# Four stacked cross-attention blocks on one core: a pace table for streams that run side by side, list-schedule durations taken from the trace, and mask terms and context loads at other places

## The chip, the cores and the metric

The kernel runs on one core of one Trainium2 chip. The core has a matrix engine (TensorE, here PE, with its weight loads as PEld), a vector engine (DVE), a scalar engine (ACT), a general engine (POOL) and a queue engine that mostly issues DMAs (SP). The metric is the device time of one execution in microseconds (us), as the median of the runs shown. One execution is also taken by the hardware profiler; durations and waits come from that one. Everything is computed in fp32.

## The reference, cut to what matters

Inputs are a batch of 4 sequences of 512 tokens with width 512 (`x`), a context of 64 tokens for each batch element, and two masks over the context. Four blocks follow each other:

```
x = L0(x, ctx):  two cross attentions (16 heads of 128, softmax over 64 context tokens and one learned key/value),
                 each h = layer_norm(x); x = x + softmax(q k^T) v wo + bo
                 then x = x + gelu(layer_norm(x) w1 + b1) w2 + b2          (w1: 512x2048)
x = L1(x, ctx):  x = x + alpha * softmax(q k^T / sqrt(512)) v wo            (one head)
x = L2(x, ctx):  16 heads of 32 over the 512 own tokens and the 64 context tokens (masked)
                 y = rmsnorm(attention + x); x = gelu(y w1 + b1) w2 + b2 + x
x = L3(x, ctx):  h = layer_norm(x); x = x + attention over the 64 context tokens (16 heads of 32, masked)
                 x = x + gelu(layer_norm(x) w1 + b1) w2 + b2
```

A masked context token gets a large negative term added to its score.

## The kernel before

**What it computes with.** Layer 0 works on tokens in the partitions. For each head, `l0_keys` (L759) makes the keys from the context and multiplies them by the query weights, so that the scores are a product of the normalized tokens with a 512 x 65 operand; `l0_values` (L826) folds values and output weights likewise. `l0_attention` (L888) forms the scores of one batch element, and `l0_tile` (L950) does softmax, transposes (L977) and the product with the folded values. After layer 0, `turn` (L1110) transposes the stream, and the rest works with channels in the partitions. `mlp` (L1034) handles two batch elements at once; its large products are made by `seven` (L1023, matmuls at L1031) with seven products in place of eight and sums on DVE or POOL (`added`, L993). `l2_attention` and `l3_attention` are the attentions of layers 2 and 3; in layer 2, DVE takes the maximum of a score bank (L1522), ACT the exponential (L1534), and PE transposes the result (L1568). `layer_norm` (L1402) is a chain: sums on DVE/POOL, a matmul with the mean (L1412), a subtraction (L1417), a square on ACT (L1398), again sums and a matmul (L1382), root and reciprocal (L1388, L1390), a product (L993) and a scale on ACT (L1423).

**What sets the order.** The order of all engines is made at build time by a class `Plan`, and each engine then runs its instructions in that order, waiting on semaphores. Each step of the kernel is recorded as an `Op` (L194) with a duration for each engine that may do it, for example `pe(2 * MM[512])` or `either(512)` (ACT or DVE). Durations come from formulas (`t_dve`, `t_act`, `t_pool`, L590 to L599) and constants (`MM`, `TR`, `ROWS`, `PAIR`, L602 to L605).

- `beside` (L276) records streams that are to run side by side. `merge` (L285) makes one order of priority of them: it always takes the next op of the stream that has done the smallest share of its own PE time (L332), provided that the live buffers stay under `FULL` blocks.
- `attempt` (L373) is a list schedule with a clock of its own: for each free engine it takes the first ready op by priority, if that lies at most `AHEAD` us of PE time (for loads `AHEAD_LOAD`) ahead of the oldest unfinished op, and if its buffers can be had. An op that has waited for memory for `PATIENCE` blocks that memory for later ones. An op more than 15 us ahead may not take the last `RESERVE` SBUF blocks (L431).
- Where no room is found, `order` (L351) repeats with a lookahead of 20 us around that place.

**The sequence of regions** (L1709 to L1774). For each pair of batch elements and each of the two attentions of layer 0, two halves of eight heads: keys and values run beside each other; in the first half the tokens then follow by themselves (load of a bias row, in the first attention loads of `x`, normalization, transposes L735, sums, and the addition of the bias row to `x` on POOL, L1730); then the attentions. After that five regions: MLP 0 of batches 0, 1 beside layer 1's projections and layer 2's context; MLP 0 of 2, 3 beside attention (layers 1 and 2) of 0, 1; MLP 2 of 0, 1 beside attention of 2, 3 and layer 3's context; MLP 2 of 2, 3 beside layer 3's attention of 0, 1; MLP 3 of 0, 1 beside layer 3's attention of 2, 3. MLP 3 of 2, 3 comes last and alone. Each MLP needs the attention of the region before it, and each attention of layers 2 and 3 the MLP before.

**Ahead of the plan** (L621 to L651), written out directly: the constants, one 512 KB DMA of the whole context on SP (L634), columns and alpha on ACT's queue, two mask loads on POOL's queue (L641, L643), and on DVE the two mask terms (L645, L649), which are read by layers 2 and 3 (L1491, L1371).

Of the kernel before, what the change touches and what calls it, by code (L numbers as in the profile page):

```python
# [192 lines left out]

class Op:  # L194
# [3 lines left out]
class Plan:  # L198
# [9 lines left out]
    PATIENCE = 3.0  # L208

    def __init__(self, sbuf, ahead, ahead_load, reserve, full):  # L210
        self.reserve, self.full = reserve, full * BLOCK
        self.sbuf = Memory(BLOCK, sbuf)
        self.psum = Memory(1024, 4)
        self.ahead, self.ahead_load = ahead, ahead_load
        self.ops, self.regions = [], []
        self.pos = 0.0
# [4 lines left out]
    def ps(self, banks=1):  # L221
        return Buf(self.psum, 512 * banks)

# [61 lines left out]
    def merge(self):  # L285


        ops, last = self.ops, {}
        for op in ops:
            for b in op.uses:  # L290
                last[id(b)] = op
        regions = [[(i, j) for i, j in parts if i < j] for parts in self.regions]
        merged, live, held = [], 0, set()

        def growth(op):
            return sum(b.size for b in op.takes if b.mem is self.sbuf and id(b) not in held)

        def put(op):
            nonlocal live
            for b in op.takes:  # L300
                if b.mem is self.sbuf and id(b) not in held:
                    held.add(id(b))
                    live += b.size
            merged.append(op)

        def drop(op):
            nonlocal live
            for b in op.uses:
                if b.mem is self.sbuf and last[id(b)] is op:
                    live -= b.size  # L310

        at = 0


        for parts in [*regions, [(None, None)]]:
            start = parts[0][0] if parts[0][0] is not None else len(ops)
            for op in ops[at:start]:
                put(op)
                drop(op)
            if parts[0][0] is None:  # L320
                break
            at = parts[-1][1]
            total = [max(sum(o.engines.get("PE", 0.0) for o in ops[i:j]), 1e-9) for i, j in parts]
            next_, gone = [i for i, _ in parts], [0.0] * len(parts)
            readers = {}
            for i, j in parts:
                for op in ops[i:j]:
                    for b in op.uses:
                        readers[id(b)] = readers.get(id(b), 0) + 1
            for _ in range(sum(j - i for i, j in parts)):  # L330
                open_ = [k for k, (_, j) in enumerate(parts) if next_[k] < j]
                open_.sort(key=lambda k: gone[k] / total[k])  # L332
                fit = [k for k in open_ if live + growth(ops[next_[k]]) <= self.full]
                k = fit[0] if fit else min(open_, key=lambda k: growth(ops[next_[k]]))
                op = ops[next_[k]]
                put(op)
                for b in op.uses:
                    readers[id(b)] -= 1
                    if b.mem is self.sbuf and not readers[id(b)]:
                        end = last[id(b)]  # L340
                        if end.n < at:
                            live -= b.size
                next_[k] += 1
                gone[k] += op.engines.get("PE", 0.0)
        self.ops = merged
        pos = 0.0
        for n, op in enumerate(merged):
            op.n, op.pos = n, pos
            pos += op.engines.get("PE", 0.0)
# [23 lines left out]
    def attempt(self, narrow):  # L373
        heaps = {e: [] for e in ("PE", "DVE", "ACT", "POOL", "SP")}
        free_at = dict.fromkeys(heaps, 0.0)
# [3 lines left out]
        events = []  # L379
# [16 lines left out]
        while left:  # L396
            progress = True
            while progress:
# [8 lines left out]
                for e, heap in heaps.items():  # L407
# [5 lines left out]
                    while heap and len(skipped) < 60:  # L413
# [9 lines left out]
                        for m in (self.sbuf, self.psum):  # L423
                            need = [b for b in op.takes if b.mem is m and b.at is None]
                            if not need:
                                continue
                            if m in blocked or not self._fits(m, need):
                                room = False
                                if m not in blocked and now >= op.ready + self.PATIENCE - 1e-9:
                                    blocked.add(m)  # L430
                            elif m is self.sbuf and op.pos > limit + 15.0:  # L431
                                room = room and len(m.free[BLOCK]) > self.reserve
# [169 lines left out]
MM = {512: 0.859, KW: 0.438, 256: 0.432}  # L602
TR = 0.109
ROWS = 1.08
PAIR = 0.96  # L605
# [13 lines left out]
def stack(nc, const, sbuf, psum, a, out):  # L619
# [8 lines left out]
    for i in range(1, 4):  # L628
# [4 lines left out]
    ctxT = const.tile([P, NC, B * T], FP, name="ctxT")  # L633
    nc.sync.dma_start(out=ctxT, in_=a["ctxT"].rearrange("(c p) s -> p c s", p=P))  # L634
# [9 lines left out]
    mterm2 = const.tile([P, B, T], FP, name="mterm2")  # L644
    nc.vector.tensor_scalar(  # L645
        mterm2.rearrange("p b s -> p (b s)"), mk_i, 0.0, -3.0e38, ALU.is_equal, ALU.mult
    )
    mterm3 = const.tile([P, B, T], FP, name="mterm3")
    nc.vector.tensor_scalar(  # L649
        mterm3.rearrange("p b s -> p (b s)"), mk_b, 0.0, LOWEST, ALU.is_equal, ALU.mult  # L650
    )  # L651

    pl = Plan(BLOCKS, AHEAD, AHEAD_LOAD, RESERVE, FULL)
    sb, ps = pl.sb, pl.ps

# [17 lines left out]
    def either(n):  # L673
        return pl.op(ACT=t_act(n), DVE=t_dve(n))
# [32 lines left out]
    def normed(src, scale, offset):  # L707
# [17 lines left out]
        for t in range(NT):  # L725
            n = sb(D)
            with either(D) as o:
                o.affine(n.v(), src[t].v(), rstd[:, t : t + 1], by[:, t : t + 1])
            xn.append(n)
        hT = []  # L730
        for c in range(NC):
            p = ps()
            with pe(4 * TR) as o:
                for t in range(NT):
                    o.transpose(p[:, t * P : (t + 1) * P], xn[t][:, c * P : (c + 1) * P], ident)  # L735
            h = sb(S)
            with either(S) as o:
                o.affine(h.v(), p.v(), col(scale, c), col(offset, c))
            hT.append(h)
# [19 lines left out]
    def l0_keys(n, half, bp):  # L759
# [6 lines left out]
        for j in range(4):  # L766
            for e in range(2):
# [6 lines left out]
                with pe(8 * TR) as o:  # L774
                    mm4(o, p[:, :P], lambda c: wk.v(NC, P)[:, c, :], lambda c: ctxT[:, c, tokens])
                with either(P) as o:
# [4 lines left out]
                for r in range(2):  # L781
                    p = ps()
                    with pe(4 * TR) as o:
# [11 lines left out]
                with pe(2 * TR) as o:  # L795
# [30 lines left out]
    def l0_values(n, half, bp):  # L826
# [6 lines left out]
        for j in range(HH):  # L833
# [5 lines left out]
            with pe(8 * TR) as o:  # L839
                mm4(o, p[:, :P], lambda c: wv.v(NC, P)[:, c, :], lambda c: ctxT[:, c, tokens])  # L840
            with either(P) as o:
# [3 lines left out]
            if j % 2:  # L845
                for i in range(2):
                    p = ps()
                    with pe(PAIR) as o:
# [101 lines left out]
    def l0_tile(half, b, t, sc, U, pb, qs):  # L950
# [14 lines left out]
        with pool(512) as o:  # L965
# [68 lines left out]
    def mlp(layer, pair, hT, func, table, b1, b2):  # L1034
# [23 lines left out]
        for q in range(F // 512):  # L1058
# [4 lines left out]
            def gelu(g, f, src):  # L1063
                g[f] = sb(S)
                with act(S, table) as o:
# [146 lines left out]
    def context_keys(layer, name):  # L1212
# [3 lines left out]
        for d in range(NC):  # L1216
# [3 lines left out]
            with either(256) as o:  # L1220
# [41 lines left out]
    def projected(w, src, name, d):  # L1262
# [5 lines left out]
        with either(S) as o:  # L1268
# [64 lines left out]
    def projected_tiles(name, T, bias, m):  # L1333


        def first(p):
            t = sb(512)
            with either(256) as o:
# [18 lines left out]
    def context_scores(q, kd, t, mterm, b, qs):  # L1357
# [12 lines left out]
        with dve(1024) as o:  # L1370
            o.scalar_tensor_tensor(  # L1371
                sc.v(H, T), p.v(H, T), qs, mterm[:, b : b + 1, :].to_broadcast([P, H, T]), ALU.mult, ALU.add
# [29 lines left out]
    def layer_norm(src, scale, offset):  # L1402
# [17 lines left out]
        for c in range(NC):  # L1420
            added(xc[c].v(), xc[c].v(), r.v(), ALU.mult, S)
            with act(S) as o:
# [6 lines left out]
    def l2_context():  # L1429
# [5 lines left out]
        with pool(256) as o:  # L1435
            o.tensor_tensor(apart[:, 256:].k(1), row[:, 256:], row[:, :256], ALU.subtract)
        bias_steps("L2_xattn_q_b")
# [3 lines left out]
    def l2_attention(b):  # L1441
# [28 lines left out]
        for g in (0, 2, 1, 3):  # L1470
# [6 lines left out]
            for i in range(NT // 2):  # L1477
# [12 lines left out]
                with dve(512) as o:  # L1490
                    o.scalar_tensor_tensor(  # L1491
                        s.v(8, T), p.v(8, T), qs, mterm2[:, b : b + 1, :].to_broadcast([P, 8, T]), ALU.mult, ALU.add
# [8 lines left out]
            for half in range(2):  # L1501
# [3 lines left out]
                for t in (2 * half, 2 * half + 1):  # L1505
# [38 lines left out]
                    with pool(256) as o:  # L1544
# [16 lines left out]
                    with pool(128) as o:  # L1561
# [67 lines left out]
    def l3_context():  # L1629
        row = load_row("L3_xattn_v_b")  # L1630
        bias_steps("L3_xattn_q_b")
        shared3.update(ckT=context_keys(3, "L3_xattn_k_b"), cv=context_values(3, row))

    def l3_attention(b):
# [10 lines left out]
        for t in range(NT):  # L1645
# [13 lines left out]
            with pool(1024) as o:  # L1659
# [50 lines left out]
    for bp, pair in enumerate(pairs):  # L1710
        for n in (1, 2):
            X, pb = {}, {}
            for half in range(2):
                made = {}
                pl.beside(
                    lambda: made.update(keys=l0_keys(n, half, bp)), lambda: made.update(U=l0_values(n, half, bp))
                )
                if not half:
                    row = load_row(f"L0_xattn_bo{n}")
                    for b in pair:  # L1720
                        if n == 1:
                            load_x(b)
                        X[b] = token_sums(normed(x[b], f"L0_xattn_ln{n}_scale", f"L0_xattn_ln{n}_offset"))
                        pb[b] = sb(P)
                        with pool(60) as o:
                            o.memset(pb[b].v(), 0.0)
                    for b in pair:
                        for t in range(NT):
                            with pool(512) as o:
                                o.tensor_tensor(x[b][t].v(), x[b][t].v(), row.v(), ALU.add)  # L1730
# [52 lines left out]
AHEAD, AHEAD_LOAD, RESERVE = 150.0, 60.0, 4  # L1783
FULL = 24
# [56 lines left out]
```

## Time and profile before

| | us |
|---|---|
| median of 3 runs (2820.83 to 2824.44) | 2823.68 |
| the profiled execution's own time | 2821.01 |
| its span, first to last instruction | 2819.2 |
| PE busy (11628 matmul instructions) | 2742.9 |
| DVE busy | 1968.8 |
| POOL busy | 1095.0 |
| ACT busy | 885.8 |
| first matmul starts | 7.37 |
| mean granted PE clock | 0.995 |

An fp32 matmul shows as two instructions. Line numbers are those of the kernel before; a helper's line (L993, L547/L548, L694) stands for many places. In lists of waits, "PE banks L1031 <- ACT arena L1423" means that the matmul at L1031 started when the ACT instruction at L1423 had ended; `arena` is SBUF, `banks` PSUM. By the starts of the matmuls, layer 0's attentions last until about 784 us, MLP 0 of batches 0, 1 until 1018, the next three MLPs' regions until 1508, 2016 and 2306, layer 3's last shared region until 2604, and the last MLP until 2814.

### The profile page before, as it was taken

To read this page: it belongs to the slowest core of one execution; us is meant where nothing else is said; L and a number is where in the kernel's file an instruction comes from. 1 tells how busy PE (TensorE), PEld (TensorE's weight loads), DVE (VectorE), ACT (ScalarE), POOL (GpSimd) and SP (SyncE) were. 2 spreads that over 40 slices of the span, in tenths; PEclk is the share of its full clock that TensorE was granted. 3 is DMA by queue.
4 is the path that set the end of the run, shared out by engine and by line. 5 is a ranking of instruction groups with operands and counts; after the bars stand their busy time and mean duration, and the time that the engine had idled before them with its cause. 6 is when DMAs were issued, how large, how long until landed. Compare 5 with 4: busy or idle time off the path is not lost. (4 is left out here: it accounts for less than half of the span.)

```text
span 2819.2 us, 33561 instructions
## 1 busy us (share of the span) xinstructions
PE 2742.9 (97%) x11628; PEld 1578.9 (56%) x11628; DVE 1968.8 (70%) x3569; ACT 885.8 (31%) x1659; POOL 1095.0 (39%) x1277
## 2 busy tenths in 40 slices
PE   8999999999999999999999999999999989999999
PEld 6667766676654455556554655555454535454444
DVE  6567566675754577777787777678886878687655
ACT  2113122131421114542462355245332213232311
POOL 4234225242322352433235232423744555545431
PEclk9999999999999999999999999999999999999999
DMA  6242142152110220110112012010211110202210
GB/s 198 88 123 65 56 154 86 47 156 83 46 53 30 71 68 8 31 52 24 38 31 79 8 31 71 20 31 16 68 45 45 39 51 30 60 16 67 68 44 30
DMA packets 229832, 163.97 MB, mean 58 GB/s; under 512 B 9072, under 2 KB 198128, under 8 KB 229664
## 3 DMA queue, kind: packets, MB, share of 16 engines
q1 hardware_dynamic: 229296, 161.52, 19.0%
q8 instruction: 93, 1.52, 0.2%
q14 instruction: 75, 0.61, 0.1%
q0 software_dynamic: 80, 0.16, 0.0%
q10 hardware_dynamic: 288, 0.15, 0.0%
HBM read 157.60 MB, written 4.19 MB: 57 GB/s over the span
## 5 line engine op out<-in xcount | busy, mean ns | idle before, releaser
L993 POOL TENSOR_TENSOR arena<-arena 128x256 f32<-128x256 f32 (+3 forms) x828 | 840.0, 1030 | 1119.9 <-ACT arena L547 202.3
L1031 PE MATMUL banks<-arena 128*128 128x512 f32 x2688 | 1212.9, 597 | 18.2 <-ACT arena L1423 12.3
L1031 PEld LDWEIGHTS banks<-arena 128*128 128x128 f32 x2688 | 499.7, 191 | 594.9 <-issue 509.6
L993 DVE TENSOR_TENSOR arena<-arena 128x512 f32<-128x512 f32 (+3 forms) x564 | 449.8, 813 | 69.7 <-ACT arena L1066 16.2
L547 ACT COPY arena<-banks 128x512 f32<-128x512 f32 (+4 forms) x464 | 227.5, 511 | 786.4 <-PE banks L1031 215.6
L548 DVE COPY arena<-banks 128x512 f32<-128x512 f32 (+2 forms) x420 | 253.7, 613 | 189.0 <-PE banks L1031 43.9
L694 PE MATMUL banks<-arena 128*128 128x512 f32 (+2 forms) x944 | 371.1, 542 | 2.3 <-DVE arena L548 0.9
L694 PEld LDWEIGHTS banks<-arena 128*128 128x128 f32 x944 | 167.8, 190 | 180.1 <-issue 167.5
L1066 ACT ACTIVATE arena<-arena,cols 128x512 f32<-128x512 f32 x192 | 137.7, 721 | 358.9 <-DVE arena L1050 176.1
L1050 DVE TENSOR_TENSOR arena<-banks,arena 128x512 f32<-128x512 f32 x240 | 164.4, 686 | 104.1 <-PE banks L1031 94.6
L1309 PE MATMUL banks<-arena 128*128 128x256 f32 x896 | 207.4, 383 | 3.4 <-ACT arena L1423 3.3
L906 PE MATMUL banks<-arena 128*128 128x260 f32 x896 | 208.5, 384 | 0.8 <-ACT arena L547 0.7
L1534 ACT ACTIVATE arena<-banks,arena 128x512 f32<-128x512 f32 x256 | 174.7, 687 | 84.6 <-DVE arena L1524 40.2
L1309 PEld LDWEIGHTS banks<-arena 128*128 128x128 f32 x896 | 170.0, 191 | 54.8 <-issue 23.2
L906 PEld LDWEIGHTS banks<-arena 128*128 128x128 f32 x896 | 164.7, 188 | 38.4 <-issue 5.8
L1522 DVE TENSOR_REDUCE arena<-banks 128x1 f32<-128x512 f32 x256 | 167.5, 680 | 12.0 <-PE banks L1511 9.9
L694 PE MATMUL banks<-ctxT,arena 128*128 128x128 f32 (+1 forms) x1152 | 164.1, 291 | 8.8 <-DMA arena<-in_L_wk 7.4
L1568 PEld LDWEIGHTS banks<-ident,arena 128*128 128x128 f32 x1024 | 116.6, 142 | 88.0 <-ACT arena L1534 32.8
L694 PEld LDWEIGHTS banks<-ctxT,arena 128*128 128x128 f32 x1152 | 148.5, 194 | 27.5 <-issue 13.6
L1568 PE MATMUL banks<-ident,arena 128*128 128x128 f32 x1024 | 140.6, 278 | 12.1 <-ACT arena L1534 11.5
L1089 DVE TENSOR_TENSOR arena<-banks,arena 128x512 f32<-128x512 f32 x144 | 98.7, 686 | 46.0 <-PE banks L1031 45.7
L985 DVE TENSOR_TENSOR arena<-banks,arena 128x512 f32<-128x512 f32 x64 | 44.2, 690 | 117.0 <-PE banks L694 114.1
(154 smaller groups left out, 2518.6 us busy)
## 6 DMA issues: line engine op xcount, KB each, us to landing
arena<-in_L_w SPq DMA_DIRECT2D x192, 256.0 KB, 3.1
arena<-in_L_wk SPq DMA_DIRECT2D x80, 256.0 KB, 4.8
arena<-in_L_wqT SPq DMA_DIRECT2D x64, 256.0 KB, 5.4
arena<-in_L_wv SPq DMA_DIRECT2D x64, 256.0 KB, 5.4
arena<-in_L_wo SPq DMA_DIRECT2D x64, 256.0 KB, 5.5
arena<-in_L_wq SPq DMA_DIRECT2D x32, 256.0 KB, 4.6
arena<-in_L_wo SPq DMA_DIRECT2D x8, 1024.0 KB, 6.0
arena<-in_L_wv SPq DMA_DIRECT2D x6, 1024.0 KB, 5.7
```

What stands on the lines that cost most here:

```text
L547: "ACT": lambda e, out, in_: e.copy(out, in_),
L548: "DVE": lambda e, out, in_: e.tensor_copy(out, in_),
L694: o.matmul(dst, lhs(c), rhs(c), start=(c == 0), stop=(c == NC - 1))
L906: o.matmul(p[:, : 2 * KP], lhs(c), rhs(c, b % 2), start=(c == 0), stop=(c == 1))
L993: o.tensor_tensor(out, x, y, op)
L1031: o.matmul(p.v(), lhs(c), rhs(c), start=(c == 0), stop=(c == 1))
L1050: o.tensor_tensor(t.v(), p.v(), y.v(), ALU.add)
L1066: o.activation(g[f].v(), src.v(), func, bias=col(b1, q * NC + f))
L1309: o.matmul(p[:, i * 256 : (i + 1) * 256], lhs(c), rhs(c), start=(c == 0), stop=(c == 1))
L1522: o.tensor_reduce(m[:, i : i + 1].k(i), banks[i].v(), AX.X, ALU.max)
L1534: o.activation(y.v(), banks[i].v(), AF.Exp, bias=nm[:, i : i + 1].k(i), scale=qs, accum_out=sums[:, i : i + 1].k(i),)
L1568: o.transpose(p[:, c * P : (c + 1) * P], e[i][:, c * P : (c + 1) * P], ident)
```

## The change

It leaves all matmuls, evictions and sums as they are and changes how they are put in order, and a few places.

1. **Pace table.** Each stream of a region gets 17 numbers: where it is to stand (in hundredths) when it has done 0/16, 1/16 ... 16/16 of its PE time. `merge` takes the stream that stands lowest. With a straight line for every stream this would be the old rule.

```
+        def stands(pace, share):
+            at = min(max(share, 0.0), 1.0) * 16
+            i = min(15, int(at))
+            lo, hi = pace[i] / 100.0, pace[i + 1] / 100.0
+            return lo + (hi - lo) * (at - i)
...
-                open_.sort(key=lambda k: gone[k] / total[k])
+                open_.sort(key=lambda k: stands(self.paces[n][k], gone[k] / total[k]))
```

Of the 13 regions' entries, the first and the last three (MLP first, then attention; in the first: keys, values, tokens):

```
+PACES = [
+    [
+        [0, 3, 16, 19, 24, 28, 34, 39, 45, 51, 55, 57, 67, 77, 80, 88, 96],
+        [8, 12, 12, 20, 24, 30, 38, 45, 50, 56, 61, 66, 69, 80, 98, 111, 114],
+        [0, 1, 8, 16, 25, 31, 38, 44, 51, 57, 64, 72, 79, 89, 90, 95, 101],
+    ],
...
+    [
+        [0, 7, 13, 19, 25, 31, 38, 43, 50, 56, 63, 69, 75, 81, 88, 94, 99],
+        [-3, 5, 13, 18, 24, 29, 37, 48, 50, 56, 63, 69, 75, 70, 87, 93, 99],
+        [-11, -5, -1, 3, 8, 10, 23, 34, 40, 45, 49, 54, 69, 83, 84, 84, 90],
+    ],
+    [
+        [0, 6, 21, 11, 24, 35, 37, 45, 49, 58, 59, 67, 72, 79, 80, 92, 96],
+        [12, 6, 15, 20, 32, 37, 46, 31, 32, 28, 48, 50, 57, 69, 82, 80, 89],
+    ],
+    [
+        [-8, -9, -7, -5, 10, 15, 23, 37, 45, 51, 62, 79, 81, 92, 97, 113, 120],
+        [-14, -14, -8, -4, 15, 22, 32, 38, 26, 39, 47, 46, 60, 92, 89, 74, 99],
+    ],
+]
```

2. **Planner's numbers.** The list schedule's engines begin at times of their own instead of 0, and five limits change:

```
+    BEGIN = {"PE": 1.0, "DVE": 3.0, "ACT": 3.0, "POOL": 3.2, "SP": 0.8}
...
-AHEAD, AHEAD_LOAD, RESERVE = 150.0, 60.0, 4
-FULL = 24
+AHEAD, AHEAD_LOAD, RESERVE = 90.0, 98.0, 2
+FULL = 22
...
+PATIENCE, NEAR = 1.75, 35.0
```

`PATIENCE` was 3.0, and `NEAR` takes the place of the 15 us beyond which the reserve holds.

3. **Durations.** Matmuls with 65 x 4 columns 0.444 instead of 0.438; short matmuls of layer 0's keys and values 0.112 (`SHORT`) instead of 0.109; an eviction with a bias 0.09 us more on ACT and half of that on DVE, one with scale and bias 0.17 and half of that; the gelu at L1066 0.725; the scale at L1423 0.81; the POOL products L966 1.06, L1545 0.62, L1562 0.3, L1660 1.92; the value pairs L850 0.04 more.

4. **Tokens of layer 0 beside keys and values.** What stood by itself after the first half's region becomes a function and a third stream of that region; its content is the same:

```
+                streams = [
+                    lambda: made.update(keys=l0_keys(n, half, bp)),
+                    lambda: made.update(U=l0_values(n, half, bp)),
+                ]
+                pl.beside(*streams, *([] if half else [l0_tokens]))
```

5. **Context in two halves, through the plan.** `ctxT` and the mask terms are fixed tiles that the plan now knows (class `Held`, which takes and gives no memory), so that their writers are ops like others. The 512 KB DMA ahead of the plan goes; for each pair of batches there is a load of its 128 context tokens:

```
-    nc.sync.dma_start(out=ctxT, in_=a["ctxT"].rearrange("(c p) s -> p c s", p=P))
...
+        two = slice(bp * P, (bp + 1) * P)
+        load(ctxT[:, :, two].k(bp), chunks(a["ctxT"])[:, :, two], NC * P)
```

6. **Mask terms.** The two DVE instructions at L645 and L649 go from the head of the kernel into `l2_context` and `l3_context`, as ops of the plan:

```
+        with dve(256) as o:
+            o.tensor_scalar(mterm2, mk_i.rearrange("p (b s) -> p b s", b=B), 0.0, -3.0e38, ALU.is_equal, ALU.mult)
...
+        with dve(256) as o:
+            o.tensor_scalar(mterm3, mk_b.rearrange("p (b s) -> p b s", b=B), 0.0, LOWEST, ALU.is_equal, ALU.mult)
```

The loads of the masks themselves stay on POOL's queue at the head.

## The prediction

> **What bounds the kernel now.** I read the busy shares first, then who PE waits for, then the granted clock at those waits, then the stages.
>
> The page's busy times and its slices (each digit a tenth of a fortieth of the span):
>
> ```profile
> PE 2742.9 (97%) x11628; PEld 1578.9 (56%) x11628; DVE 1968.8 (70%) x3569; ACT 885.8 (31%) x1659; POOL 1095.0 (39%) x1277
> ...
> PE   8999999999999999999999999999999989999999
> ```
>
> PE is busy for 2742.9 of 2819.2 us; no other engine is near. DMA moves 58 GB/s in the mean, and 275 to 305 in the first 40 us. So only time in which PE does nothing, or runs slowly, can be won. The page shows 76.3 us of it, but a matmul that ends before a wait counts as busy until its modelled end. So I also took, from the trace's starts, the time from one matmul's start to the next, and subtracted the lower quartile of the same group (0.429 us for 512 columns, 0.216 for 256, 0.109 to 0.112 for 128). The floor is 2665.1 us, 143.7 us are lost between matmuls, 7.4 pass before the first and 4.7 after the last. Of the 143.7, 94.5 lie in 142 waits of over 0.15 us; the other 49 are crumbs that an order hardly reaches.
>
> Who PE waited for (waiter, releaser, us in total, times, longest):
>
> ```profile
> PE banks L1031 <- ACT arena L1423: 12.3, 2, 9.5
> PE banks L1568 <- ACT arena L1534: 11.5, 14, 2.3
> PE banks L694 <- DMA arena<-in_L_wk: 7.4, 1, 7.4
> PE banks L1511 <- ACT arena L1534: 7.0, 8, 1.5
> PE banks L1382 <- POOL arena L993: 3.8, 1, 3.8
> PE banks L1309 <- ACT arena L1423: 3.3, 3, 2.2
> ```
>
> Two kinds matter. L1423 and L1382 are the ends and the middle of a layer norm: the next region's MLP (L1031) has to wait for it. L1534 is an exponential of layer 2's attention, for which the transposes L1568 wait, often and briefly. L694 is the very first matmul.
>
> The stages, with PE's busy time as second number (length, then PE, PEld, DVE, ACT, POOL, granted clock, DMA):
>
> ```profile
> 0.00:54.70 54.70, 43.93 (x296) 33.77 (x297) 29.50 (x70) 13.78 (x29) 15.51 (x46) 1.00 0.74 232
> 54.70:784.00 729.30, 724.08 (x3672) 495.55 (x3671) 470.65 (x988) 184.22 (x349) 268.07 (x381) 1.00 0.30 90
> 784.00:1038.00 254.00, 252.95 (x715) 127.84 (x714) 143.83 (x224) 40.31 (x59) 87.92 (x77) 1.00 0.16 50
> 1038.00:2016.00 978.00, 947.71 (x4836) 545.13 (x4835) 738.00 (x1541) 428.47 (x919) 353.12 (x448) 1.00 0.13 39
> 2016.00:2604.00 588.00, 568.90 (x1599) 283.99 (x1598) 452.94 (x566) 175.14 (x242) 302.92 (x273) 0.99 0.15 42
> 2604.00:2819.20 215.20, 205.29 (x518) 92.59 (x516) 133.87 (x184) 43.89 (x65) 67.43 (x57) 0.99 0.15 47
> ```
>
> By starts the six lose 9.8, 24.2, 2.4, 64.6, 31.6 and 9.4 us (rounded, 142), and their waits over 0.15 us are 4.6, 7.6, 1.7, 45.4, 27.0 and 8.2. Layer 0 (to 784) is nearly closed. Two thirds lie from 1038 on, where MLP and attention run beside each other.
>
> The worst place, the chain at the border between the last two shared regions, by PE's lines of the timeline:
>
> ```profile
> 2314.21 1.13 PE L1412 MATMUL banks<-arena,mean 128*128 128x512 f32 x2
> ...
> 2324.87 10.67 PE L1031 MATMUL banks<-arena 128*128 128x512 f32 x19 [9.53 <-ACT arena L1423]
> ```
>
> Two of the stretches that I asked for, in the columns of the stages:
>
> ```profile
> 2319.20:2329.40 10.20, 4.53 (x6) 1.95 (x7) 9.79 (x10) 4.30 (x6) 8.99 (x7) 0.50 0.00 0
> 2489.90:2493.20 3.30, 3.30 (x10) 2.59 (x9) 2.45 (x4) 0.00 (x0) 2.59 (x3) 0.50 0.00 0
> ```
>
> The MLP of batches 2, 3 and the attention of 0, 1 end together at 2314; then nothing is left for PE while a layer norm runs through ACT, DVE (a reciprocal of 3.34 us) and POOL. PE idles 9.53 us and gets half the clock until 2329.4. After a wait of 2.22 us at 2488 the clock is halved too, for 3.4 us. There are six such stretches: near 1456, 1828, 2029, 2319, 2490, 2626. Five of 3.4 us cost 1.7 each, the long one, in which PE ran from 2324.9, 2.3: 10.8 us.
>
> **The change, part by part.**
>
> *Work itself.* No matmul, eviction or sum is added or removed; one DMA is added (the context in two). So the floor of 2665.1 us stays, and the sum is about lost time alone.
>
> *Start.* The first matmul waits until 7.37 us for a weight that queues behind all 512 KB of context; half of that is now loaded later. 256 KB at the 275 GB/s of the first 20 us are 0.95 us. The two mask terms (L645, L649; 0.29 us each) leave DVE's queue: the second waits 0.99 us for its mask and starts at 10.06, and the first key's shift (L553) stands behind it at 10.27, though its matmuls end at 9.41: 0.7 us with the 0.2 that such a step takes. They go beside the MLP of 784 to 1038, where DVE is busy 143.8 of 254 us: nothing there; without that cover 0.3 us each. The second context half is one SP issue (0.4 to 0.5 us) amid 256 KB loads, needed about 400 us later: nothing. l0_tokens becomes a third stream: it takes along a row load and, for the first pass, eight loads of x (256 KB each, 5.6 us of SP issue now at 27.8), eight statistics on DVE (L713), eight POOL additions (1.32 us each) per pass and the transposes L735. Now its DVE and ACT work falls in 40 to 60 us, where DVE is busy 17.7 of 20 and PE idles 1.8; earlier it finds DVE at 11.3 of 20. Against it: 2.3 MB earlier among weights when DMA is busy 0.93 is 7.5 us of transfer in front of weights at 305 GB/s. Bounds: the stage loses 9.8 us and 7.4 before it, of which at best half goes, -8; at worst two thirds of the 7.5 come through, +5. The weights still lead in the pace table (third stream at 0, 1, 8 against 0, 3, 16 where low goes first), so I am near the gain: **-4**.
>
> *Rest of layer 0.* The waits of L977, L694, L735 (up to 1.0 us) around 451 to 461 and 647 are where tokens now stand alone. They add to 7.6 us; half goes: **-4** (0 to -8). 784 to 1038: **0**.
>
> *Borders from 2016 on.* The pace table lets attention run ahead: in the region of the MLP of layer 3, its attention's last point is 99, where the MLP passes 99 at share 0.88; in the region before, 89 against 0.92. An MLP is 448 matmuls of 0.429, 192 us, so 23 and 15 us of MLP remain as cover, against a chain of 23.6 us (2301.3 to 2324.9), of which 9.5 was bare. What goes if the cover holds: waits of 9.70, 4.01, 2.90, 2.38, 1.05 and 1.05 by starts, 21.1, and 7.4 of clock (2.3 and three times 1.7): 28.5. I take three quarters, since the attention that goes ahead leaves less beside the MLP's own short waits: **-22** (-33 to +5).
>
> The clock is shown by the rows above. [...]
>
> *Layer 2's attention, 1038 to 2016.* Waits of 45.4 us in 74 places, mean 0.6, and 3.4 of clock within. Here gain comes from a finer order: durations now like the rows (0.725 for the gelu, row L1066 721 ns; 1.06 for L966, row 1051; 0.112 for short matmuls; 1.92 for L1660, row 1956), a shorter patience, other paces. Bounds: nothing or +10, where an instruction is put ahead of one that is then late; -40, nearly all waits. What limits it is that the same form still varies: L993 on POOL with 512 columns takes 1456 ns in the mean, L966 of the same width 1051, so an order exact to 0.1 us isn't kept. I take 45%: **-20**.
>
> *Lookahead 150 to 90, loads 60 to 98, FULL 22, reserve 2.* 90 us of PE work still exceeds the 23.6 us chain; loads land in 3.1 to 8.1 us against 60 already: **0**.
>
> Sum: -4 - 4 - 20 - 22 = -50. Span 2819.2 - 50 = 2769.2; the profiled execution has 1.8 us around it (2821.0): 2771.0. The median before, 2823.68, is 2.7 above that execution: **2773.7, say 2773 us**, 1.8% faster.
>
> **The rivals.**
>
> *A: borders alone.* The fine waits come back elsewhere, because DVE (738 of 978 us) and the shared exponentials set the pace from 1038 to 2016. For: 14 waits of L1568 on L1534, each ended by ACT right behind DVE. Against: ACT is busy 428 of 978 us, so a head start of one tile would do. Gain 4 + 22 = 26 with little else: 2798 (2790 to 2816).
>
> *B: nearly closed.* All waits over 0.15 us but a fifth go: 0.8 x 94.5 = 75, plus start: 2745 (2728 to 2757).
>
> *C: the table changes little.* Priority alone moves, PE is 97% busy, and the ready list gives the same order: 2823 (2818 to 2829).
>
> *D: slower, by memory.* With reserve 2 instead of 4 and loads 98 us ahead, the planner runs out of room in some place and repeats with a lookahead of 20 us there; the 23.6 us chain then lies bare at six places, as many as have a halved clock now: 9.5 + 2.3 at each is 70.8, less the 28.5 and the 8.2 (2.43, 2.35, 3.4) lost there now, is +34: 2858. It decides once four places or more are so hit. Against: FULL falls from 24 to 22 blocks, which asks for less. A milder case gives 2830 to 2840.
>
> **How the numbers follow.** Forecast (2757 to 2790) 0.46; A 0.22; B 0.19; C 0.05; D 0.08. Faster by over 0.2% (about what a measurement of this kernel can tell from no change) is all of the first three: 0.87; C 0.05; D 0.08. The range leaves out C, D and the lower part of B (0.06): 2738 to 2816.
>
> **What would show it.** Right: PE's floor the same; the waits on L1423 and L1382 under 8 us in total instead of 19.4; at most two half-clock stretches after 1000 us; first matmul near 6.4 us; L906 starting before 52 us; lost time from 1038 to 2016 near 45 us. Wrong: a new wait of PE on a DMA of wk in the first 60 us (the tokens' loads), L1568's and L1511's waits still above 15 us (A), or long waits at new borders (D). A floor that moves, through the clock or missing overlap of packed matmuls, would break the whole sum.

## The result and the profile after

The changed kernel takes 2774.5 us in the median (2771.5 to 2778.5 in four runs), the kernel before beside it 2822.64; the ratio is 0.983 with a 95% interval of 0.9813 to 0.9847. The forecast was 2773. The profiled execution took 2772.95 us, its span is 2771.1. In lines after the change L1031 is L1054, L1423 is L1446, L1382 is L1405, L1412 is L1435, L1534 is L1559, L1568 is L1593, L1511 is L1536, L694 is L717, L993 is L1016.

The page of the changed kernel, busy times and PE's slices:

```profile
PE 2730.7 (99%) x11628; PEld 1578.9 (57%) x11628; DVE 1929.8 (70%) x3516; ACT 889.5 (32%) x1663; POOL 1144.9 (41%) x1325
...
PE   8999999999999999999999999999999999999999
```

The same 11628 matmuls stand in a span that is 48 us shorter. By the starts of the matmuls, with the quartiles of the kernel before, the floor is again 2665.1 us; lost between matmuls are 95.3 us instead of 142 (2819.2 less the floor, 7.4 in front and 4.7 behind; the 143.7 of the prediction is 1.7 too much). The waits of over 0.15 us are 92 with 50.9 us instead of 142 with 94.5.

Who PE waited for, longest first:

```profile
PE banks L717 <- DMA arena<-in_L_wk: 6.0, 1, 6.0
PE banks L1536 <- ACT arena L1559: 4.7, 6, 2.0
PE banks L1054 <- ACT arena L1559: 4.0, 3, 2.3
PE banks L1593 <- ACT arena L1559: 3.5, 5, 1.4
PE banks L717 <- DVE arena L737: 3.2, 1, 3.2
PE banks L1435 <- POOL arena L1016: 1.4, 1, 1.4
```

The waits on the end and the middle of a layer norm (19.4 us before) have gone from the head of the list. Behind the first weight, the exponentials are now first, and there is a new wait of 3.2 us at the start. The view puts it down to a statistic of the tokens (L737). But these are the matmuls of the first value weight `wv`, whose load is issued behind a row and four loads of `x` (the queue is shown below) and lands at 14.49 us (the second key's weight lands at 17.59); the matmuls start at 14.63. In e4, with the same order on the queue, the same wait is put down to that load:

```profile
PE banks L717 <- DMA arena<-in_L_wv: 4.0, 1, 4.0
```

The stages of the changed kernel, cut where the same work ends:

```profile
0.00:56.40 56.40, 45.42 (x288) 34.05 (x288) 32.33 (x74) 18.54 (x37) 25.20 (x50) 1.00 0.97 295
56.40:782.00 725.60, 725.21 (x3697) 498.69 (x3694) 457.24 (x993) 175.46 (x334) 270.23 (x391) 1.00 0.30 89
782.00:1033.00 251.00, 250.87 (x684) 124.75 (x683) 145.90 (x213) 38.00 (x57) 90.57 (x81) 1.00 0.18 52
1033.00:1993.00 960.00, 942.46 (x4853) 548.27 (x4853) 722.36 (x1511) 430.25 (x929) 360.12 (x464) 1.00 0.13 37
1993.00:2562.00 569.00, 564.93 (x1601) 281.33 (x1600) 446.80 (x556) 191.68 (x255) 331.42 (x291) 1.00 0.16 45
2562.00:2771.10 209.10, 201.82 (x515) 91.81 (x513) 125.20 (x174) 35.57 (x53) 67.33 (x53) 1.00 0.13 41
```

A table by equal work is sharper. I sum the floor over the matmuls in order and compare the times at which 37.6, 742.6, 994, 1908 and 2665 us of it are done (the ends of the start, layer 0, the first MLP, layer 2's attention, and all). Each column is the time gained (-) or lost in that stretch against before, in the profiled executions (which lie up to 4 us beside their medians). The last two are the median against the changed kernel's, and what the kernel's own list schedule reckons at build time against the same (the planner's clock, not a measurement).

| run | median | start | layer 0 | MLP | 994 to 1908 | from 1908 | median, vs 2774.5 | planner |
|---|---|---|---|---|---|---|---|---|
| changed | 2774.5 | +2.7 | -5.8 | -1.8 | -18.2 | -25.0 | | |
| e1 straight paces, last two | 2777.4 | +1.9 | -5.9 | -1.7 | -11.9 | -22.6 | +2.9 | +1 |
| e2 table shifted, a | 2794.0 | +0.4 | -5.8 | -1.6 | +2.5 | -21.7 | +19.5 | +24 |
| e3 table shifted, b | 2819.3 | -0.8 | -3.9 | -1.8 | +14.8 | -7.8 | +44.8 | +46 |
| e4 old limits | 2817.5 | +2.7 | -5.9 | -1.6 | -3.6 | +6.1 | +43.0 | +40 |
| e5 old reserve rule | 2804.1 | +2.2 | -5.8 | +0.7 | -10.8 | -3.9 | +29.6 | +31 |
| e6 before, new reserve rule | 2802.8 | +0.3 | -5.7 | +0.9 | -1.8 | -12.0 | | |
| e7 old durations | 2778.4 | +3.0 | -10.2 | -1.3 | -18.6 | -15.9 | +3.9 | |
| e8 first tokens alone | 2773.2 | -4.0 | -4.8 | -2.2 | -14.4 | -23.1 | -1.3 | +1 |
| e9 no table | 2793.2 | +1.4 | -2.9 | -0.3 | -2.2 | -23.1 | +18.7 | +25 |
| e10 context and masks alone | 2814.5 | -1.1 | -3.0 | +0.8 | -1.1 | -1.6 | | |
| e11 searched on | 2767.0 | -4.6 | -6.5 | -2.0 | -23.4 | -21.6 | -7.5 | -13 |
| e12 old rule for loads | 2807.2 | +1.0 | -4.8 | -2.0 | -5.4 | -1.1 | +32.7 | +32 |

### The profile page after: what moved, and what is told of

Its sections match the earlier page's. It is cut to its first block, busy times and chain, and to the rows that moved or that the text cites. A ratio compares the mean times of both kernels' runs of the same rounds, so it can differ in the third digit from the quotient of the medians.

```text
span 2771.1 us, 33551 instructions
## 1 busy us (share of the span) xinstructions
PE 2730.7 (99%) x11628; PEld 1578.9 (57%) x11628; DVE 1929.8 (70%) x3516; ACT 889.5 (32%) x1663; POOL 1144.9 (41%) x1325
## 5 line engine op out<-in xcount | busy, mean ns | idle before, releaser
L1016 POOL TENSOR_TENSOR arena<-arena 128x256 f32<-128x256 f32 (+3 forms) x876 | 887.8, 1029 | 1089.5 <-DVE arena L576 202.1
L1054 PE MATMUL banks<-arena 128*128 128x512 f32 x2688 | 1203.8, 595 | 7.4 <-ACT arena L1559 4.0
L1054 PEld LDWEIGHTS banks<-arena 128*128 128x128 f32 x2688 | 497.4, 190 | 584.5 <-issue 508.2
L575 ACT COPY arena<-banks 128x512 f32<-128x512 f32 (+3 forms) x489 | 242.7, 513 | 786.4 <-PE banks L1054 277.6
L1016 DVE TENSOR_TENSOR arena<-arena 128x512 f32<-128x512 f32 (+3 forms) x516 | 419.2, 824 | 70.1 <-POOL arena L1016 20.3
L717 PE MATMUL banks<-arena 128*128 128x512 f32 (+2 forms) x944 | 368.2, 542 | 0.3
L576 DVE COPY arena<-banks 128x512 f32<-128x512 f32 (+3 forms) x395 | 237.1, 607 | 163.1 <-PE banks L1054 49.8
L717 PEld LDWEIGHTS banks<-arena 128*128 128x128 f32 x944 | 167.8, 190 | 180.3 <-issue 173.9
L1559 ACT ACTIVATE arena<-banks,arena 128x512 f32<-128x512 f32 x256 | 174.7, 687 | 96.5 <-DVE arena L1549 55.1
L717 PE MATMUL banks<-ctxT,arena 128*128 128x128 f32 (+1 forms) x1152 | 167.4, 294 | 10.2 <-DMA arena<-in_L_wk 6.0
L717 PEld LDWEIGHTS banks<-ctxT,arena 128*128 128x128 f32 x1152 | 149.6, 195 | 33.0 <-issue 13.1
L1593 PEld LDWEIGHTS banks<-ident,arena 128*128 128x128 f32 x1024 | 118.0, 142 | 77.5 <-issue 34.8
L1593 PE MATMUL banks<-ident,arena 128*128 128x128 f32 x1024 | 140.0, 276 | 4.7 <-ACT arena L1559 3.5
```

Of the source, the lines that this page charges most:

```text
L575: "ACT": lambda e, out, in_: e.copy(out, in_),
L576: "DVE": lambda e, out, in_: e.tensor_copy(out, in_),
L717: o.matmul(dst, lhs(c), rhs(c), start=(c == 0), stop=(c == NC - 1))
L1016: o.tensor_tensor(out, x, y, op)
L1054: o.matmul(p.v(), lhs(c), rhs(c), start=(c == 0), stop=(c == 1))
L1559: o.activation(y.v(), banks[i].v(), AF.Exp, bias=nm[:, i : i + 1].k(i), scale=qs, accum_out=sums[:, i : i + 1].k(i),)
```

## The experiments

**Do the paces cover the borders?** Theory 1 is the prediction's: attention runs ahead of the MLP and leaves it as cover. Theory 2: the table is fitted to one order, and the order as a whole is what counts.

e1, straight lines in the last two shared regions:

```
+PACES[11:] = [[[100 * i / 16 for i in range(17)] for _ in r] for r in PACES[11:]]
```

> The changed kernel with straight paces in the last two shared regions (MLP 2 of batches 2, 3 and MLP 3 of 0, 1, each beside layer 3's attention). Theory 1, as predicted: the paces there let attention run ahead and so cover the layer norm; without them the waits on the layer norm's end and some halved clock come back, 15 to 25 us: 2790 to 2800 us. Theory 2: the gain at the borders comes from the order as a whole (lookahead, reserve, durations), and the paces there matter little: 2770 to 2780 us, PE's waits on the norm's end still under 8 us.

2777.4 us (ratio 0.9839, 0.9824 to 0.9854). From 1908 on 22.6 of the 25.0 us remain. In the changed kernel attention did lead: its last norm's first matmul stands 18.7 and 29.9 us ahead of the MLP's last matmul at the two borders, 3.9 and -0.4 before. In e1 the leads are again 3.9 and -0.4, and the borders are closed all the same. Theory 1, by which the leads are needed, falls.

e2 and e3, each number of the table moved by -2 to +2 (two draws; e3 differs in the seed alone):

```
+_r = random.Random(1)
+PACES = [[[p + _r.choice((-2, -1, 0, 1, 2)) for p in t] for t in r] for r in PACES]
```

> The changed kernel with every number of the pace table moved at random by -2 to +2 hundredths. Theory 1, the table expresses which stream should lead and when: so small a shift keeps the covers, and the time stays within 6 us of 2774.5. Theory 2, the table is fitted to one order, and what it gains lies in the fit, not in a rule: half or more of the 48 us goes, 2795 to 2815 us, with the loss spread over many short waits and not at the borders. The kernel's own planner reckons 24 us more than for the changed kernel.

> The same with another draw of -2 to +2 hundredths. Theory 1: within 6 us of 2774.5. Theory 2: as the last, and as the kernel's planner reckons 46 us more than for the changed kernel, near 2815 to 2825; if the planner's clock says nothing of the chip, this run and the one before fall in either order.

2794.0 (0.9898, 0.9883 to 0.9912) and 2819.3 (0.9992, 0.9983 to 1.0002). e2 is a little better than its forecast of 2795 to 2815. A shift that leaves the two leads about as they were (17.0 and 30.6 us in e2, 24.1 and 31.5 in e3) costs 19.5 and 44.8 us, nearly all of it from 994 to 1908 in e2, and there and behind in e3. The order of loss is that of the planner's clock.

**Are the limits worth nothing?** e4, the changed kernel with the five limits of before and 15 us for `NEAR`:

```
-AHEAD, AHEAD_LOAD, RESERVE = 90.0, 98.0, 2
-FULL = 22
-PATIENCE, NEAR = 1.75, 35.0
+AHEAD, AHEAD_LOAD, RESERVE = 150.0, 60.0, 4
+FULL = 24
+PATIENCE, NEAR = 3.0, 15.0
```

> The changed kernel with the limits of before (lookahead 150, loads 60, reserve 4, FULL 24, patience 3, 15 us). Theory 1: the limits are worth nothing by themselves, as predicted: 2770 to 2782 us. Theory 2: any limit is part of the fit, and the planner reckons 40 us more: 2805 to 2820 us.

2817.5 (0.9979, 0.9969 to 0.9988): 43 us more, 31 of them from 1908 on. PE's matmuls at the border of e4, and the granted clock there:

```profile
2291.70 15.37 PE L1054 MATMUL banks<-arena 128*128 128x512 f32 x35
2309.30 1.12 PE L1435 MATMUL banks<-arena,mean 128*128 128x512 f32 x2 [2.23 <-POOL arena L1016]
2319.81 2.07 PE L1405 MATMUL banks<-arena,mean 128*128 128x512 f32 x2 [9.39 <-POOL arena L1016]
2321.68 10.88 PE L1054 MATMUL banks<-arena 128*128 128x512 f32 x22
```

```profile
2311.00:2324.00 13.00, 4.19 (x5) 1.80 (x6) 12.83 (x12) 3.11 (x5) 10.79 (x9) 0.50 0.00 1
```

Attention leads by 18.4 us here, as in the changed kernel, and yet PE idles 9.39 us at half the clock: the lead alone isn't the cover. So theory 3: the rule on the last SBUF blocks decides. An op more than `NEAR` us ahead may not take them, and the next MLP's weights and sums are such ops.

e5, only that rule as before; e6, the kernel before with three numbers alone, the rule's two and the lookahead (`AHEAD`):

```
e5:
-AHEAD, AHEAD_LOAD, RESERVE = 90.0, 98.0, 2
+AHEAD, AHEAD_LOAD, RESERVE = 90.0, 98.0, 4
...
-PATIENCE, NEAR = 1.75, 35.0
+PATIENCE, NEAR = 1.75, 15.0
e6:
-                            elif m is self.sbuf and op.pos > limit + 15.0:
+                            elif m is self.sbuf and op.pos > limit + 35.0:
...
-AHEAD, AHEAD_LOAD, RESERVE = 150.0, 60.0, 4
+AHEAD, AHEAD_LOAD, RESERVE = 90.0, 60.0, 2
```

> The changed kernel with only the reserve rule of before: the last 4 blocks of SBUF, not 2, are kept from ops more than 15 us, not 35, ahead. Theory 3, formed from the last four runs (old limits bring the half clock at the borders back, straight paces there don't): the borders are bare because the ops that could cover them lie more than 15 us ahead and are refused memory. Then the stretch from 1900 us on loses 15 to 25 us more, with halved clock again near 2290 to 2480: 2795 to 2808 us. Theory 2 (fit only): a loss of any size, not at the borders in particular. Theory 1: nothing, under 2782 us. The kernel's planner reckons 31 us more than for the changed kernel.

> The kernel before with three numbers alone: 15 us to 35, reserve 4 to 2, lookahead 150 to 90. No pace table, old durations, tokens and context as before. Theory 3: the borders from 2000 us on gain 8 to 15 us and the whole 15 to 25, without any table: 2797 to 2808 us. Theory 2: the limits are worth something only with the table fitted to them: within 6 us of 2822. The planner reckons 21 us less than for before.

2804.1 (0.9938, 0.9923 to 0.9953) and 2802.8 (0.993, 0.9914 to 0.9947), both as theory 3 had it. e5 loses 21 us of the 25 from 1908 on, e6 gains 12 there and 19.3 in all, with no table at all. What the lookahead adds in e6 no run separates.

**What is worth the rest?** e9, everything changed but the table (straight paces everywhere; FULL 23, since at 22 the planner finds no room):

```
+PACES = [[[100 * i / 16 for i in range(17)] for _ in r] for r in PACES]
-FULL = 22
+FULL = 23
```

> The changed kernel with straight paces in all 13 regions (each stream at its own share, the old rule) and FULL at 23, since the planner finds no room at 22; limits, durations, tokens, context and masks as changed. Theory 3 (the reserve rule closes the borders, the table only finds a good order elsewhere): from 1900 us on the gain over before stays at 15 to 25 us, attention leads the MLP at the border by no more than before (near 4 us), and what is lost against the changed kernel lies between 1000 and 1900 us: 2792 to 2802 us. Theory 1 (the table's leads are the cover): the borders are bare again, from 1900 us on no gain, 2810 us and more.

2793.2 (0.989, 0.9874 to 0.9907). From 1908 on the gain stays whole at 23.1, with leads of 3.9 and -0.4; from 994 to 1908 it is 2.2 instead of 18.2. PE at the border of e9:

```profile
2292.32 1.02 PE L1435 MATMUL banks<-arena,mean 128*128 128x512 f32 x2
2293.17 8.75 PE L1054 MATMUL banks<-arena 128*128 128x512 f32 x20
2301.76 1.02 PE L1405 MATMUL banks<-arena,mean 128*128 128x512 f32 x2
2302.61 1.97 PE L1054 MATMUL banks<-arena 128*128 128x512 f32 x4
2304.42 1.02 PE L1435 MATMUL banks<-arena,mean 128*128 128x512 f32 x2
2305.28 12.18 PE L1054 MATMUL banks<-arena 128*128 128x512 f32 x28
```

Up to 2304 this is the sequence of the kernel before (x20, x4, then the next norm at 2314). There PE then had nothing; here it has 28 more. They belong to the next MLP, though the norm of its batch 1 isn't done: two of the seven products of `seven`, a11 b11 and a12 b21, need batch 0 alone, and there is such a pair for each block of `w1` in SBUF (by the plan's order, the 28 also hold the first product of two blocks of `w2`, whose input needs batch 0 alone).

The changed kernel gets over the same border in another way. These are the last scales of batch 1's norm on ACT, before, in the changed kernel, in e9 and in e4:

```profile
2323.30 1.52 ACT L1423 ACTIVATE arena<-arena,cols 128x512 f32<-128x512 f32 x2 [0.70 <-DVE arena L993]
2277.77 1.52 ACT L1446 ACTIVATE arena<-arena,cols 128x512 f32<-128x512 f32 x2 [0.17 <-POOL arena L1016]
2312.68 1.52 ACT L1446 ACTIVATE arena<-arena,cols 128x512 f32<-128x512 f32 x2 [0.16 <-POOL arena L1016]
2300.48 1.52 ACT L1446 ACTIVATE arena<-arena,cols 128x512 f32<-128x512 f32 x2 [0.16 <-POOL arena L1016]
```

The last matmul of MLP 2 of 2, 3 starts at 2305.6, 2276.4, 2296.2 and 2299.4. So the norm ends 19.2 us behind it before, 2.9 us in the changed kernel, 18.0 in e9 and 2.6 in e4 (0.6 in e5). In the changed kernel the lead does bring the norm in time, and by the plan's order the third product behind the border, s4 b22, already uses batch 1. e9 (like e1) does without it. e4 and e5 have the norm and stay bare, because sums on POOL come late: 9.39 us of wait in e4, 5.86 in e5.

I also counted in the traces the weight loads of the MLPs issued by 10 us before the last matmul of MLP 2 of 2, 3, beyond that MLP's own: 6 before, 2 in e4, 8 in e5, 6 in e6 and e10; 14 in the changed kernel, 10 in e1, 12 in e9. And L1054's instructions in the 20 us behind that matmul: 17 before, 16 in e4, 28 in e5, 27 in e6, 29 in e10; 39, 42 and 42.

e12, the old rule for the loads alone:

```
-                            elif m is self.sbuf and op.pos > limit + self.near:
-                                room = room and len(m.free[BLOCK]) > self.reserve
+                            elif m is self.sbuf and op.pos > limit + (15.0 if op.load else 35.0):
+                                room = room and len(m.free[BLOCK]) > (4 if op.load else 2)
```

> The changed kernel with the old reserve rule (15 us, 4 blocks) for the weight loads alone; the computing ops keep the new one. Theory 3, narrower: what the old rule withholds at the borders is the next MLP's weights, so that its first sums come late; then the stretch from 1900 us on loses 12 to 22 us again: 2795 to 2810 us. If the rule acts through the computing ops alone, the borders stay closed, and what is lost (a new draw) lies before 1900 us.

2807.2 (0.9946, 0.9929 to 0.9962); from 1908 on 23.9 of the 25.0 us are gone, a little over the forecast, but not at that border: 38 instructions of the MLP stand in those 20 us, with 6 loads ahead. So the count of loads doesn't tell whether a border is covered. By the same sum, the work that lay from 2290 to 2345 us before gains 10.0 us in the changed kernel and 8.8 in e12, 1.9 in e5, and loses 3.2 in e4. e5 and e12 differ in the rule for the computing ops alone, so at that border the old rule acts through the computing ops, the sums among them, rather than through the loads. (e10, with the old rule throughout, gains 5.7 there: another order does a part of it too.) What e12 loses lies elsewhere, at waits on another norm's end (4.4 us) and on DVE (4.8 us). Whether the loads that are kept back cause it, or another order, isn't shown.

e7, the durations of before in the planner (the eleven constants and formulas of point 3 put back):

> The changed kernel with the durations of before in the planner, all else as changed. If the durations matter on the chip by themselves, the order that the planner finds with the old ones, though it looks as good to the planner (by its old clock), runs worse: 8 to 20 us more, 2783 to 2795 us, mainly in short waits on the exponentials between 1000 and 2000 us. If they don't: 2770 to 2780 us, or a loss like that of the shifted tables, since any other order is a new draw.

2778.4 (0.9845, 0.983 to 0.986), 3.9 more, within what another order may do. The new durations are worth little by themselves.

**The start.** e8, tokens by themselves in the first region only; e10, the kernel before with context halves and mask terms alone:

```
e8:
-                pl.beside(*streams, *([] if half else [l0_tokens]))
+                pl.beside(*streams, *([] if half or not (n + bp > 1) else [l0_tokens]))
+                if not half and n + bp == 1:
+                    l0_tokens()
```

> The changed kernel with the tokens by themselves in the very first region only, as before; the seven others stay as changed. The trace of the changed kernel shows four loads of x and a row between the first weights, the statistics on DVE ahead of the second key's shift, and PE 5.5 us behind the kernel before at equal work (10 us of it). If those loads are the cause, at 10 us of PE work it is 4 to 6 us earlier, and with a later order as good as the changed one: 2768 to 2774 us. If the cause is the slow clock alone, the start stays as it is.

> The kernel before with only the context in two halves through the plan and the mask terms in layers 2 and 3: straight paces, old limits, old durations, tokens by themselves, engines beginning at 0. As predicted for this part, the first matmul is 1.0 to 1.5 us earlier and the first key's shift 0.7 more: at 37.6 us of PE work 1 to 2 us gained, nothing later but what a slightly different order brings: 2816 to 2825 us. Theory 2 would call even the rest a new draw, of up to 10 us either way.

e8: 2773.2 (0.9827, 0.9813 to 0.9842). The start is 6.7 us better than in the changed kernel, and about 6 of it are given back later, in another order. e10: 2814.5 (0.9971, 0.9959 to 0.9983), 8 us less than before and under its forecast of 2816 to 2825: 1.1 us of it lie at the start, as forecast; the other 5 that its profiled execution shows lie in small steps in a different order, of which I have no cause.

The changed kernel's SP queue and PE at the start:

```profile
1.80 0.50 SPq L701 DMA_DIRECT2D arena<-in_L_wqT  x1
2.34 0.44 SPq L701 DMA_DIRECT2D arena<-in_rows  x1
2.82 4.20 SPq L701 DMA_DIRECT2D arena<-in_x  x4
7.06 1.43 SPq L701 DMA_DIRECT2D arena<-in_L_wv  x1
```

```profile
6.03 2.05 PE L717 MATMUL banks<-ctxT,arena 128*128 128x128 f32 x8 [6.03 <-DMA arena<-in_L_wk]
8.90 2.07 PE L808 MATMUL banks<-arena 128*128 128x130 f32 x8 [0.82 <-DMA arena<-in_L_wqT]
10.77 0.64 PE L819 MATMUL banks<-arena,cols 128*128 128x130 f32 x2
14.63 2.05 PE L717 MATMUL banks<-ctxT,arena 128*128 128x128 f32 x8 [3.22 <-DVE arena L737]
```

The first matmul is 1.3 us earlier, but a row and four loads of x go out behind the first key's two weights and ahead of all others, the first value's matmuls start at 14.63 instead of 11.71, and eight still take 2.05 us where they take 1.05 at full clock (from 26.59 on; granted clock 1.00).

**A faster version.** e11 starts from e8 and changes the table further in small random steps, keeping what lowers the planner's clock (patience 2.25).

> The first region's tokens by themselves, as in the eighth run, and the pace table changed further in small random steps, each kept when the planner's own clock fell; patience 2.25, other limits as changed. The planner reckons 14 us less than for the eighth run (2773.2 us). Theory 2 in full (the time follows the planner's clock, whatever the numbers of the table mean): 2757 to 2763 us, with the gain between 1000 and 1900 us. If the planner's clock is worth nothing at this scale: 2768 to 2778 us.

2767.0 us (0.9803, 0.9788 to 0.9817), the fastest here, 55 us under the kernel before beside it. That lies between its two forecasts (2757 to 2763, and 2768 to 2778). Its four runs (2763.0 to 2768.9) lie below all four of the changed kernel, though the two intervals of the ratio overlap. Against e8 it won 6 of the 14 us that the planner reckoned, 9 of them between 994 and 1908, with some given back behind.

## Why the prediction was right, and where it wasn't

- **Floor:** unchanged, 2665.1 us. Right.
- **Start, -4:** wrong in sign, +2.7. The parts on context and masks held (first matmul at 6.03 against some 6.4, first shift at 8.12 instead of 10.27; e10's -1.1). The step that failed is "The weights still lead in the pace table, so I am near the gain". The numbers given beside it say the opposite: the lowest goes first, and the tokens' 0, 1, 8 lie below the keys' 0, 3, 16 and the values' 8, 12, 12; and a row, loads of x and statistics have no PE time, so they don't move their stream on at all. SP's queue shows row and x in front of `wv`. With the tokens by themselves (e8) the start is -4.0; so taking them along costs 6.7 us, over the bound of 5 that I had set.
- **Rest of layer 0, -4; first MLP, 0:** -5.8 and -1.8. Right in mechanism, the first a little small.
- **Borders, -22:** the size was right (-25.0), the cause only in part. The pace table does give the leads that I worked out (18.7 and 29.9 us against 15 and 23), and in the changed kernel the norm ends in time at the first of them (2.9 us behind the MLP instead of 19.2). But the leads are not needed, since e1 and e9 close the borders without them, and not enough, since e4 leaves the border bare with them. The step that failed is the one put at nothing, "Lookahead 150 to 90, loads 60 to 98, FULL 22, reserve 2": the limits cost 43 us when undone (e4), the reserve rule alone 29.6 (e5), and three numbers give the kernel before 19.3 (e6). I had set 90 us against a chain of 23.6 and not asked what an op beyond 15 us may take from memory.
- **Layer 2's attention, -20:** -18.2, and 46.4 us lost there against the 45 forecast. The reason "durations now like the rows" failed (e7). The table brings it (e9 has 2.2 without), but as one order found by fitting: a shift of two hundredths takes all of it and more (e2, e3).
- **Rival D, memory:** its condition came, its price didn't. The plan of the changed kernel does run out of room and repeats with the lookahead of 20 us, five times around four places, all in layer 2's attention (1083 to 1783 us of PE work); the plan of the kernel before never does. The norms' chains at the borders lie elsewhere, so the +34 stayed away; what the repeats cost in layer 2's attention no run separates. The rule that D feared, with its smaller reserve, is the main gain.
- Of the signs named, the waits on the norm, one halved stretch after 1000 us beside the last, and the first matmul came as said; L906 before 52 us did not (56.4). Of the signs of being wrong, a new wait on a weight behind the tokens' loads came too, though on `wv` and not on `wk`.

So 2773 against 2774.5 is partly luck: an error of 6.7 us at the start is made up by 3.0 at the borders, 1.8 in the rest of layer 0, 1.8 in the MLP and the rounding, less 1.8 in layer 2.

What stays open: e3 loses 17 us behind 1908 with the new rule in force, half of it at the border at 2010, where a wait of 8.8 us follows and only 12 instructions of the MLP stand in the 20 us behind, so an unlucky order can cost there too; the rule is the main cause by the sum of the runs (with it -7.8 to -25.0 in nine kernels, the one before as base 0; with the old one, in e12 for the loads alone, -3.9 to +6.1 in four). Which withheld op is the decisive one at the other borders isn't settled, nor what reserve and distance (`NEAR`) are worth each. e4 costs 13 us more than e5: the other limits have no run of their own, and neither have `BEGIN` and the tokens of the later regions.

## What to carry to other kernels

When a hand-made list schedule leaves the main engine bare at a stage border, ask first what the scheduler's memory rules keep from being fetched ahead, and count in the trace how many of the next stage's matmuls run in the first 20 us behind the border. The number of its loads that are out didn't tell here (6 with 17 matmul instructions, 6 with 38), and a stream's lead was of no use without the sums that the next stage starts from. A table fitted to one order is worth what the fit finds, and a shift of 2% in it undid 19.5 and 44.8 of 48 us here, so judge such a table by a disturbed copy as well. Loads that a step takes along belong behind those that the first busy engine waits for (ahead of them, the tokens' cost 6.7 us here, by e8).

## What the runs showed of the hardware that I had not expected

Whether a wait of PE of 2 to 3 us was followed by a lower clock was not the same at every place. In the kernel before, four waits of 2.18 to 2.73 us, which ended at 1454.72, 1826.45, 2488.48 and 2626.11, were each followed by half the clock for 3.41 us, as was one of 3.84 us that ended at 2028.75; around one of 9.53 us that ended at 2324.87 it was half for 10.24 us, from 2319.20 on. In the changed kernel's profile a wait of 2.01 us on an exponential, which ended at 1938.17, was followed by half the clock for 3.41 us from 1938.44, and one of 2.29 us on another, which ended at 1424.67, was not (1.00 from 1424 to 1428). The changed kernel's four runs took 2771.5, 2772.95, 2776.05 and 2778.47 us with mean granted clocks of 1.000, 0.999, 0.998 and 0.997. What decides whether such a wait costs clock isn't shown.

At the start, the record of the granted clock begins, at full speed, at 15.20 us before, 7.8 us after the first matmul, and only at 23.56 us in the changed kernel, 17.5 us after it, with a wait of 3.22 us in between (the 1.00 in the stage rows counts the time ahead of the record as full). Around these times the matmuls became faster: eight instructions of 128 columns took 1.92 us from 11.71 and 1.05 from 20.30 before, 2.08 us from 19.65 and 1.05 from 26.59 in the changed kernel. In e8, without the tokens' loads and with a wait of 2.13 us, eight took 2.05 us both from 5.64 and from 9.82.
